# Order of work in the first pass of layer 0's self attention: exponentials two rounds sooner, context keys in every second round, their maxima last, parts by a two-operand maximum

## The chip, the cores and the metric

The kernel runs on one core of one Trainium2 chip. A core has engines with queues of their own: TensorE multiplies matrices (PE in the profile, with its weight loads as PEld) and writes to PSUM; VectorE (DVE), ScalarE (ACT) and GpSimd (POOL) work elementwise or reduce; SyncE (SP) mostly issues DMA transfers. Each engine takes its instructions in order and waits on semaphores for the others. The metric is the device time of one launch in microseconds; 1% of it here is 21.9 us.

## The reference

Four transformer blocks run one after the other on x, 8 batches of 256 tokens with 320 channels, with a context of 120 tokens. The change touches the first block, whose attentions quantise their operands. Cut to that block's attention:

```python
def fq_sym(x, bits=8):                       # symmetric, one step for the whole tensor
    qmax = 2.0 ** (bits - 1) - 1.0
    delta = jnp.maximum(jnp.max(jnp.abs(x)), 1e-08) / qmax
    return jnp.clip(jnp.round(x / delta), -qmax - 1.0, qmax) * delta

def fq_zero(x, bits=8):                      # for weights of the softmax, all positive
    levels = 2.0 ** bits - 1.0
    delta = jnp.maximum(jnp.max(x), 1e-08) / levels
    return jnp.clip(jnp.round(x / delta), 0.0, levels) * delta

def attention(x, ctx, Wq, Wk, Wv, Wo, bo, heads):      # 20 heads of 16
    q, k, v = fq_sym(x @ Wq), fq_sym(ctx @ Wk), fq_sym(ctx @ Wv)
    ...                                                # to [b, heads, tokens, 16]
    scores = jnp.einsum('bhnd,bhmd->bhnm', q, k) * dh ** (-0.5)
    w = fq_zero(jax.nn.softmax(scores, axis=-1))
    out = jnp.einsum('bhnm,bhmd->bhnd', w, v)
    return out.transpose(0, 2, 1, 3).reshape(b, n, c) @ Wo + bo

h = layer_norm(x, ln1_g, ln1_b)
x = x + attention(h, h, Wq1, Wk1, Wv1, Wo1, bo1, heads)                               # self
x = x + attention(layer_norm(x, ln2_g, ln2_b), ctx, Wq2, Wk2, Wv2, Wo2, bo2, heads)   # cross
x = x + geglu_ff(layer_norm(x, ln3_g, ln3_b), Wff1, bff1, Wff2, bff2)
```

The three steps `delta` of q, k and v need maxima over the whole tensor, and so does the step of the softmax weights. The largest weight of a row of scores is 1 over its sum of exponentials once the row's maximum is taken off, so the step of the weights needs the smallest such sum of all rows. That is why each attention goes over its scores twice: the first pass finds row maxima and sums, the second pass computes the weights again, rounds them and multiplies them with v.

## The kernel before

Everything stays on the chip; x lies in SBUF for the whole kernel. Layer 0's attentions are two objects of the class `Quant`, `s` (self) and `c` (cross). Heads lie in 5 groups of four, each head in 32 rows. The order of work comes from three places. Generators emit their instructions in steps, and `weave` takes one step of each live generator per turn; a turn is called a round here, and each generator has a round in which it starts. The framework then places waits and orders instructions within each engine's queue, by its own estimate, around that order; `behind` (line 293) ties an instruction's place to that of another without a wait. Pools of buffers set the rest: three PSUM pairs (`pair`, tile pf, 128x2x512 floats), two PSUM banks (`bank`, pa).

Self attention begins with `project_all`, which makes q, k and v of the 8 batches (the weights were loaded by `load`, q first, then k, v and o). `steps` turns the three maxima into steps. `whole` rounds q and k of a batch to whole numbers, batch 0 on VectorE and GpSimd, batches 1 and 2 on ScalarE (`whole_by_act`), batches 3 to 7 on GpSimd (`whole_all(3)`), which goes on with v (`whole_v`, lines 1391 to 1404) and adds a bias to x. The first pass then weaves four generators (line 1669), with n = 10 units per batch, a unit being one group of heads and one half of its four heads:

- `tops_all`, from round 0. One unit per round: four score products (L1453) into a PSUM pair, and a negated maximum over the keys of each row on VectorE (L1456). After a batch's tenth unit its maxima, 128x40 numbers, are split into three bf16 parts whose sum is the number: a cast (L1473), a subtraction (L1475), cast, subtraction, cast. In the third unit of the next batch (`i == 2`) TensorE transposes the parts (L1464) and ScalarE copies them to `nTs` (L1467).
- `sums_all`, from round n + 4 = 14. One unit per round: `exps` computes the scores of the unit again with keys in the rows (L1497), adds the maxima out of `nTs` by a second product with a selecting matrix, also L1497, and ScalarE takes exponentials (L1504). Products with `place` (L1519) add them over the keys; per batch, ScalarE copies the sums (L1524) and VectorE takes their minimum (L1525).
- `whole_all(3)`, from round 0, on GpSimd.
- `c.keys_all`, from round 7: the eight batches' keys of the cross attention, one per round: six products of the context with Wk2 (L120, two passes each) into a PSUM pair and a copy by ScalarE (L1274).

`c.top` then takes each key tile's absolute maximum on VectorE (L1214), `weight_steps` computes the step of the weights, and the second pass follows (`out_all`). The cross attention later runs the same `tops_all` and `sums_all` with n = 6 units and its sums from round n + 4 = 10; its own `whole_all` runs beside.

Of the kernel before, what the change touches and what calls it, by code (L numbers as in the profile page):

```python
# [14 lines left out]
ALU = mybir.AluOpType  # L15
# [4 lines left out]
B, N, C = 8, 256, 320  # L20
# [1171 lines left out]
class Quant:  # L1192
# [18 lines left out]


    def top(self, i, b, src):
        self.k.nc.vector.tensor_reduce(  # L1214
            self.am[: src.shape[0], i, b : b + 1], src, AX.XY if i == 2 else AX.X, ALU.max, apply_absolute_value=True
        )

# [220 lines left out]
    def tops_all(self):  # L1438

        k, nc, nk = self.k, self.k.nc, self.nk  # L1440
        held = None
        for b in range(B + 1):
            if b < B:
                negm = k.small.tile([P, 4, G, TPB], F32, tag="negm", name="negm")
            for i, (gs, h) in enumerate(self.units):
                if b < B:
                    s = k.pair()
                    for n, g in enumerate(gs):
                        for t in range(TPB):
                            for j in range(2):  # L1450
                                kt, q = self.operands(b, g, 2 * h + j)
                                o = (n * TPB + t) * nk
                                nc.tensor.matmul(  # L1453
                                    s[:, j, o : o + nk], q[:, t * P : (t + 1) * P], kt, start=True, stop=True
                                )
                    nc.vector.tensor_reduce(  # L1456
                        negm[:, 2 * h : 2 * h + 2, gs[0] : gs[-1] + 1, :].rearrange("p j g t -> p j (g t)"),
                        s[:, :, : len(gs) * TPB * nk].rearrange("p j (t k) -> p j t k", k=nk),
                        AX.X, ALU.max, negate=True,
                    )  # L1460
                if i == 2 and held is not None:
                    ps = k.ps_a.tile([P, 1024], BF16, tag="a", name="pt")
                    for t in range(TPB):
                        nc.tensor.transpose(  # L1464
                            ps[:, t * P : (t + 1) * P], held[:, t].rearrange("p j r -> p (j r)"), k.ident16
                        )
                    nc.scalar.copy(k.nTs[:, b - 1, :], ps[:, :N])  # L1467
                if i == len(self.units) - 1 and b < B:
                    held = k.npx
                    src = negm.rearrange("p j g t -> p t j g")  # L1470
                    for n in range(3):
                        part = held[:, :, :, G * n : G * (n + 1)]
                        nc.vector.tensor_copy(part, src)  # L1473
                        if n < 2:
                            nc.vector.tensor_tensor(src, src, part, ALU.subtract)  # L1475
                yield
                if b == B and i == 2:
                    return

    def exps(self, b, gs, heads, kind):  # L1480
# [156 lines left out]
def kernel(ctx: ExitStack, tc: tile.TileContext, a, out):  # L1637
    k = Kernel(ctx, tc, a, out)
    with ExitStack() as es:
        k.open_flow(es)  # L1640

        def load(layer, q, kk, v, o, row):
            plain = layer == "L0"
            w = {"q": k.weight_q("q", f"{layer}_xattn_{q}", q == "Wq2")}
            if kk is not None:
                w["k"] = (k.weight_q if plain else k.weight_k)("k", f"{layer}_xattn_{kk}")
                w["v"] = k.weight_v("v", f"{layer}_xattn_{v}")
            if o is not None:
                w["o"] = k.weight_o("o", f"{layer}_xattn_{o}")
            return w, k.bias_row(k.fk, row)  # L1650

        w, brow, loaded, w3 = {}, {}, {}, {}
        dram = es.enter_context(tc.tile_pool(name="ahead", bufs=1, space=bass.MemoryType.DRAM))
        ff = ExitStack()
        with tc.tile_pool(name="l0", bufs=1) as pool:
            k.open_quant(pool)
            with tc.tile_pool(name="l0_keys", bufs=1, side="right") as kpool:
                s = Quant(k, pool, kpool, 0, *load("L0", "Wq1", "Wk1", "Wv1", "Wo1", 0), False)
                k.load_ctx()
                s.project_all()  # L1660
                c = Quant(k, pool, pool, 1, *load("L0", "Wq2", "Wk2", "Wv2", "Wo2", 1), True)
                s.steps()
                for _ in s.whole(0, True):
                    pass

                s.whole_by_act(1)
                s.whole_by_act(2)
                n = len(s.units)
                k.weave((0, s.tops_all()), (n + 4, s.sums_all()), (0, s.whole_all(3)), (7, c.keys_all()))
                for b in range(B):  # L1670
                    c.top(1, b, c.kk[b])
                s.weight_steps()
                v = c.values_all()
                for _ in range(2):
                    next(v)
                k.weave((0, s.out_all()), (8, c.queries_all()), (5 * B + 4, islice(v, 3)))
            fp = ff.enter_context(tc.tile_pool(name="w_ff1", bufs=1, side="right"))
            context = ExitStack()
            k.open_context(context.enter_context(tc.tile_pool(name="context", bufs=1, side="right")), dram)
            ahead = k.context_steps()  # L1680
            next(ahead)
            loaded["w"] = [k.weight_ff1(fp, "L0_xattn_Wff1")]
            brow["ff0"] = k.bias_row(k.fk, 2)
            w["self"], brow["self"] = load("L1", "q1", "k1", "v1", "o1_w", 3)
            c.steps()
            next(ahead)
            for _ in c.whole(0, True):
                pass
            n = len(c.units)
            k.weave(  # L1690
                (0, c.tops_all()), (n + 4, c.sums_all()), (0, c.whole_all()), (5, v),
                (1, k.paced(islice(ahead, 20), 1)),
            )
            c.weight_steps()

            def rest():
                yield from ahead
                context.close()
                with tc.tile_pool(name="ahead_last", bufs=1, side="right") as pool:
                    yield from k.weights_last_steps(pool, dram)  # L1700

            k.weave((0, c.out_all()), (0, k.paced(rest(), 1)))
            fp2 = ff.enter_context(tc.tile_pool(name="w_ff2", bufs=1, side="right"))
            loaded["w"].append(k.weight(fp2, "ff2", "L0_xattn_Wff2"))
# [118 lines left out]
```

## Time and profile before

| what | value |
|---|---|
| median of 3 runs | 2194.03 us (2193.57 to 2208.99) |
| span of the profiled execution | 2202.1 us |
| busy share: PE, DVE, ACT, POOL | 92%, 51%, 38%, 15% |
| first score product of the first pass | 108.07 us |
| GpSimd busy in it | 109.3 to 188 us |
| last maxima, last sum of exponentials | 240.80 us, 257.92 us |

The stage by stretches: the microseconds in which each engine was busy, and the mean clock that TensorE was granted (1.00 is full).

| stretch, us | length | PE | DVE | ACT | POOL | clock |
|---|---|---|---|---|---|---|
| 108 to 133 | 25 | 21.33 | 22.45 | 11.03 | 23.60 | 0.77 |
| 133 to 188 | 55 | 43.86 | 43.92 | 33.78 | 54.96 | 0.84 |
| 188 to 240 | 52 | 47.56 | 45.51 | 39.63 | 0.00 | 0.97 |
| 240 to 258 | 18 | 17.62 | 2.20 | 16.60 | 0.00 | 1.00 |

A row of the timeline gives the start, the duration, engine, line and operation, the tile written and the one read, and how many instructions it merges; the bracket is idle time before it and what ended it. [...] The chain of waits is followed back from the last instruction to whatever released each, so its shares say which work stood on the path.

### The profile page before, as it was taken

How to read it: one execution, taken by the hardware profiler on the slowest of the kernel's cores; microseconds unless marked ns; L12 is line 12 of the kernel's file. 1: busy time of each engine (PE TensorE's matmuls, PEld its weight loads, DVE VectorE, ACT ScalarE, POOL GpSimd, SP SyncE). 2: the span in 40 equal slices, each digit the busy share in tenths (PEclk: the TensorE clock that was granted, in tenths of full speed). 3: DMA queues.
4: the chain of work that ended last, by engine and by line, in shares of the span. 5: the costliest groups of instructions: out<-in, count | busy, mean ns of one | idle time of the engine just before them, and what ended most of it. 6: DMA issues, size and time to landing. Idle time of an engine off the chain costs nothing.

```text
span 2202.1 us, 38254 instructions
## 1 busy us (share of the span) xinstructions
PE 2036.4 (92%) x16415; PEld 1194.6 (54%) x16415; DVE 1112.6 (51%) x1698; ACT 833.3 (38%) x1259; POOL 330.5 (15%) x358
## 2 busy tenths in 40 slices
PE   7888889898889999999999998899999999999997
PEld 5643345554444465465555555544555655666664
DVE  5388687445651222235555567621121666546565
ACT  3456888367542121124444444311201333222221
POOL 3194033723010000000000010100000100000100
PEclk9989889898899999999999999999999999999999
DMA  4000000642120000020000101100000120000000
GB/s 118 20 12 2 2 1 1 174 111 57 52 85 14 1 0 1 1 93 2 2 2 22 28 25 36 47 1 0 1 0 1 24 68 23 19 16 26 23 19 16
DMA packets 79303, 63.21 MB, mean 29 GB/s; under 512 B 48410, under 2 KB 68318, under 8 KB 78622
## 3 DMA queue, kind: packets, MB, share of 16 engines
q1 hardware_dynamic: 75070, 57.06, 9.4%
q10 hardware_dynamic: 4064, 3.71, 0.6%
q8 instruction: 129, 2.11, 0.4%
q14 instruction: 40, 0.33, 0.0%
HBM read 42.61 MB, written 17.37 MB: 27 GB/s over the span
## 4 chain that ended last, share of the span: by engine, by line
PE 73%; DVE 15%; issue 4%; ACT 4%; POOL 2%; DMA 2%; SPq 0%; ACTq 0%; DVEq 0%; POOLq 0%
PE pf L594 13%; PE pf L120 11%; PE pf L132 9%; PE pa L120 7%; PE pa L456 6%; PE pf L439 4%; PE pa L594 3%; PE pf L139 3%; DVE negm L1456 3%; PE pf L394 3%; PE pf L736 3%; DVE rs L464 3%; PE pf L1497 2%; PE pa L1519 2%; DVE negm L401 2%
## 5 line engine op out<-in xcount | busy, mean ns | idle before, releaser
L445 ACT ACTIVATE e<-pf 128x1024 f32<-128x1024 f32 (+2 forms) x176 | 158.5, 946 | 220.1 <-PE pf L439 213.1
L401 DVE TENSOR_REDUCE negm<-pf 128x4 f32<-128x1024 f32 (+4 forms) x224 | 188.1, 887 | 97.9 <-PE pf L394 97.9
L594 PE MATMUL pf<-xTf,ff 128*128 128x512 f32 x512 | 230.8, 597 | 6.2 <-DVE negm L401 5.2
L464 DVE RECIPROCAL rs<-pa 128x256 f32<-128x256 f32 x88 | 152.3, 1745 | 143.5 <-PE pa L456 143.5
L1504 ACT ACTIVATE e<-pf,sc_s 128x1024 f32<-128x1024 f32 x160 | 169.8, 1118 | 48.7 <-PE pf L1497 44.8
L1456 DVE TENSOR_REDUCE negm<-pf 128x4 f32<-128x1024 f32 (+2 forms) x128 | 143.3, 1151 | 69.6 <-PE pf L1453 58.2
L619 DVE SCALAR_TENSOR_TENSOR hT<-pf,cols_sb,gl 128x512 f32<-128x512 f32 x64 | 48.0, 751 | 256.4 <-ACT gl L618 254.1
L120 PE MATMUL pf<-ff,hT 128*128 128x320 f32 x640 | 174.4, 434 | 0.0
L594 PEld LDWEIGHTS pf<-xTf,ff 128*128 128x128 f32 x512 | 94.3, 190 | 125.4 <-issue 118.5
L120 PEld LDWEIGHTS pf<-ff,hT 128*128 128x128 f32 x640 | 120.9, 190 | 55.5 <-issue 6.1
L618 ACT ACTIVATE gl<-pf,cols_sb 128x512 f32<-128x512 f32 x64 | 44.0, 689 | 247.8 <-PE pf L594 247.8
L439 PE MATMUL pf<-qT,kT 32*128 32x256 f32 (+1 forms) x1280 | 122.1, 410 | 9.1 <-DVE negm L401 7.5
L394 PE MATMUL pf<-kT,qT 32*128 32x120 f32 (+1 forms) x1920 | 113.1, 326 | 18.6 <-ACT e L445 18.3
L487 POOL TENSOR_TENSOR xb<-x_sb,brow 128x640 f32<-128x640 f32 x24 | 37.0, 1543 | 563.8 <-DVE x_sb L493 555.4
L120 PE MATMUL pa<-o,oT 128*128 128x320 f32 x352 | 105.7, 441 | 15.2 <-DVE oT L465 15.2
L394 PEld LDWEIGHTS pf<-kT,qT 32*128 32x128 f32 x1920 | 83.0, 186 | 58.4 <-ACT e L445 27.5
L647 POOL TENSOR_TENSOR xb<-x_sb,brow 128x640 f32<-128x640 f32 x16 | 25.0, 1563 | 573.8 <-DVE x_sb L652 528.2
L1497 PE MATMUL pf<-Q,K 32*128 32x256 bf16 (+1 forms) x960 | 90.5, 295 | 21.7 <-DVE negm L1456 11.5
L456 PE MATMUL pa<-e,v 128*32 128x256 f32 (+1 forms) x1280 | 106.1, 391 | 2.3 <-ACT e L445 1.7
L1606 DVE TENSOR_SCALAR w<-e 128x1024 bf16<-128x1024 f32 (+2 forms) x128 | 89.2, 703 | 32.3 <-ACT e L1504 31.1
L132 PE MATMUL pf<-xT,q 128*128 128x256 f32 x384 | 100.5, 391 | 0.4 <-ACT e L445 0.2
L439 PEld LDWEIGHTS pf<-qT,kT 32*128 32x128 f32 (+1 forms) x1280 | 68.4, 182 | 55.5 <-DVE negm L401 26.9
(291 smaller groups left out, 3439.2 us busy)
## 6 DMA issues: line engine op xcount, KB each, us to landing
ff<-in_L_xattn_Wff_dram SPq DMA_DIRECT2D x1, 2560.0 KB
qT<-nT SPq DMA_DIRECT2D x160, 4.0 KB
ff<-in_L_xattn_ff_w_dram SPq DMA_DIRECT2D x1, 2560.0 KB
out_dram<-x_sb SPq DMA_DIRECT2D x16, 160.0 KB
kd_cross<-kst SPq DMA_DIRECT2D x8, 300.0 KB
vd_cross<-vst SPq DMA_DIRECT2D x8, 300.0 KB
vd_both<-vst SPq DMA_DIRECT2D x8, 300.0 KB
kT<-kd_cross SPq DMA_DIRECT2D x8, 300.0 KB
```

The lines of the kernel that those rows point to most:

```text
L120: self.nc.tensor.matmul(out, l, r, start=i == 0, stop=i == len(pairs) - 1)
L132: self.nc.tensor.matmul(o, *t[c], start=start and c == 0, stop=stop and c == n - 1, skip_group_check=True)
L394: nc.tensor.matmul(s[j // 2][:, j % 2, o : o + nk], qT[r : r + PAD, g, t * P : (t + 1) * P], kT[r : r + PAD, g, :nk], start=True, stop=True,)
L401: nc.vector.tensor_reduce(negm[:, n, 2 * i : 2 * i + 2, g0 : g0 + len(gs), :].rearrange("p j g t -> p j (g t)"), sv[:, :, :, k0:k1], AX.X, ...
L439: nc.tensor.matmul(s[j // 2][:ks, j % 2, o : o + N], kT[r : r + PAD, g, c * ks : (c + 1) * ks], qT[r : r + PAD, g, :], start=True, stop=True,)
L445: nc.scalar.activation(e[:ks, 2 * i : 2 * i + 2, :n], s[i][:ks, :, :n], AF.Exp, scale=scale)
L456: nc.tensor.matmul(o[j * PAD : (j + 1) * PAD, what * N : (what + 1) * N], w, es[g][:ks, j, c * N : (c + 1) * N], start=first and c == 0 an ...
L464: nc.vector.reciprocal(rs, o[:, N:])
L594: ins = nc.tensor.matmul(*args, **kw)
L1456: nc.vector.tensor_reduce(negm[:, 2 * h : 2 * h + 2, gs[0] : gs[-1] + 1, :].rearrange("p j g t -> p j (g t)"), s[:, :, : len(gs) * TPB * n ...
L1497: nc.tensor.matmul(s[at // 2][:ks, at % 2, o : o + N], l, m, start=not shift and o == 0, stop=shift and o + N == n, skip_group_check=True,)
L1504: nc.scalar.activation(e[:ks, :, :n], ps[:ks, :, :n], AF.Exp, scale=self.sc[:ks, 9:10])
```

## The change

Six edits:

1. In `load`, k's weight is loaded ahead of q's, with the memsets that go with it, for every layer that loads both here.
2. `c.keys_all` starts in round 2 and takes every second round (`paced(..., 1)` yields once more after each step), so in rounds 2, 4, ..., 16 instead of 7 to 14.
3. `sums_all` of the self attention starts in round n + 2 = 12.
4. In `tops_all` the transposes are emitted in the second unit of the next batch (`i == 1`), for both attentions, and the generator ends a round earlier.
5. The three bf16 parts are written by a `tensor_tensor` maximum of the source with itself in place of a `tensor_copy`, for both attentions.
6. The eight maxima of the context keys (`c.top`) are tied behind the last maxima of scores (`self.reduced`), so that VectorE runs them after those.

```diff
     def top(self, i, b, src):
-        self.k.nc.vector.tensor_reduce(
+        return self.k.nc.vector.tensor_reduce(
             self.am[: src.shape[0], i, b : b + 1], src, AX.XY if i == 2 else AX.X, ALU.max, apply_absolute_value=True
         )
...
-                    nc.vector.tensor_reduce(
+                    self.reduced = nc.vector.tensor_reduce(
                         negm[:, 2 * h : 2 * h + 2, gs[0] : gs[-1] + 1, :].rearrange("p j g t -> p j (g t)"),
...
-                if i == 2 and held is not None:
+                if i == 1 and held is not None:
                     ps = k.ps_a.tile([P, 1024], BF16, tag="a", name="pt")
...
                     for n in range(3):
                         part = held[:, :, :, G * n : G * (n + 1)]
-                        nc.vector.tensor_copy(part, src)
+                        nc.vector.tensor_tensor(part, src, src, ALU.max)
                         if n < 2:
                             nc.vector.tensor_tensor(src, src, part, ALU.subtract)
                 yield
-                if b == B and i == 2:
+                if b == B and i == 1:
                     return
...
-            w = {"q": k.weight_q("q", f"{layer}_xattn_{q}", q == "Wq2")}
+            w = {}
             if kk is not None:
                 w["k"] = (k.weight_q if plain else k.weight_k)("k", f"{layer}_xattn_{kk}")
+            w["q"] = k.weight_q("q", f"{layer}_xattn_{q}", q == "Wq2")
+            if kk is not None:
                 w["v"] = k.weight_v("v", f"{layer}_xattn_{v}")
...
-                k.weave((0, s.tops_all()), (n + 4, s.sums_all()), (0, s.whole_all(3)), (7, c.keys_all()))
+                k.weave((0, s.tops_all()), (n + 2, s.sums_all()), (0, s.whole_all(3)), (2, k.paced(c.keys_all(), 1)))
                 for b in range(B):
-                    c.top(1, b, c.kk[b])
+                    k.behind(c.top(1, b, c.kk[b]), s.reduced)
                 s.weight_steps()
```

## The prediction

> **What bounds the kernel now.** The page first: TensorE is busy for 92% of the span, so a gain has to shorten the path that feeds it, and the change touches one stage only. That stage is the first pass of layer 0's self attention, from the first score product at 108.07 us to the last sum of exponentials at 257.92 us: 150 of 2202 us, 6.8%. I call one turn of its weave a round; 80 rounds of maxima (10 for each of 8 batches) overlap with 80 rounds of exponentials that start 14 rounds later. The chain of waits of that stretch comes next, its first line being shares by line:
>
> ```profile
> by line: DVE negm L1456 31.8%; PE pa L1519 19.2%; PE pf L1497 15.0%; DVE npx L1473 8.6%; PE pf L1453 7.7%; PE pf L120 5.7%; ACT e L1504 5.2%; DVE negm L1475 2.3%; issue 1.6%; PE pt L1464 1.4%; DVE am_c L1214 1.2%; DVE K L1358 0.4%; ACT sums
> ```
>
> The maxima on VectorE (L1456) carry the most, and L1473, a cast of 128x40 values, carries 8.6% of 150 us = 12.9 us. The busy table by stretches (L1473 alone) says where:
>
> ```profile
> 108.00:133.00 25.00, 1.72 (x3) 0.77 0.00 1
> 133.00:188.00 55.00, 11.00 (x9) 0.84 0.10 12
> 188.00:240.00 52.00, 1.70 (x9) 0.97 0.01 2
> 240.00:258.00 18.00, 0.58 (x3) 1.00 0.01 2
> ```
>
> The columns are the stretch, its length, the casts' busy time with their number, and the granted clock. After 188 us a cast takes 0.19 us; before it twelve take 12.72 us, 10.4 more than 12 x 0.19. GpSimd works without a break from 109.3 to 188 us and not at all from there to 240 us. The timeline of VectorE and GpSimd shows one of these casts:
>
> ```profile
> 160.46 0.34 DVE L1473 CAST npx<-negm 128x40 bf16<-128x40 f32 x1
> 160.83 0.23 DVE L1475 TENSOR_TENSOR negm<-negm,npx 128x40 f32<-128x40 f32 x1
> ...
> 161.74 1.57 POOL L1391 TENSOR_SCALAR tv<-V,sc_s 128x640 f32<-128x640 f32 x2
> 162.62 2.95 DVE L1473 CAST npx<-negm 128x40 bf16<-128x40 f32 x1
> 163.26 2.26 POOL L1394 MEMSET V<- 128x1280 bf16 x2
> ```
>
> The cast of 162.62 ends at 165.57, as the memset ends at 165.52. The subtraction between the casts (L1475, two SBUF operands, the same 128x40) takes 0.23 us beside a GpSimd TENSOR_SCALAR. First parts of a batch begin at 141.98, 160.46, 176.79, 196.77, 211.46, 226.14 and 240.84 us: a clean batch takes 14.69 us, the three contended ones 18.48, 16.33 and 19.98, 10.7 more than three clean ones.
>
> **The changed parts.** Sums are against the 2202.1 us span; the median of the runs shown is 2194.03, 0.4% less, and I subtract the same microseconds from it.
>
> *Cast to maximum.* All 24 operations of the stage (and 24 in the cross pass) become two-operand operations on one source. No row shows this very form; the nearest is L1475: eight in 120-188 us take 2.32 us, 0.10 each above 0.19, and the single delayed one (144.37, 0.85 us) ends with GpSimd's L1352 (144.28 to 145.18). Lower bound: no wait at all, -10.7; upper: no better than the casts, 0 (worse is a rival below). I take L1475, nearest in operands, shape and time: 3 parts x 0.10 = 0.3 of each contended batch stays, so -10.7 + 0.9 = **-9.8**. Two stretches of half clock, 146.9-150.4 and 181.1-191.3, follow long casts and are in those intervals.
>
> [...]
>
> *Transposes a round earlier.* They now stand in TensorE's queue after the scores of the next batch's second unit and before an exponentials' group, where before they stood one round on. They wait for the fifth part operation, which VectorE runs after the first unit's maxima. In the clean batch at 211.46 those maxima end at 213.49, the part at 213.58, and the group went at 213.54, released by the same maxima. Now it waits for the part (0.04 to 0.1 more) and the two transposes (0.22): 0.3 us later. Transposes leave a later place worth 0.22, so 0 to 0.3, taken 0.2, for six batches: **+1.2**. Behind them queue the exponentials and ScalarE. In the cross pass the parts of 476.80 end at 477.91 and the second unit's scores run at 480.0: 2 us of cover, 0; its casts' excess is off the chain, 0.
>
> *Keys in every second round from round 2, their maxima last, exponentials at round 12.* Before, six rounds of maxima at 1.13 us are followed by eight that each carry a key product:
>
> ```profile
> 124.91 1.60 PE L120 MATMUL pf<-ctxT,k 128*128 128x120 f32 x12
> ...
> 125.07 0.53 DVE L1473 CAST npx<-negm 128x40 bf16<-128x40 f32 x1
> 125.50 1.21 DVE L1456 TENSOR_REDUCE negm<-pf 128x4 f32<-128x1024 f32 x1
> ```
>
> There a round costs 1.85 to 2.2 us, for 1.60 + 0.39 of TensorE and 1.13 + 0.44 (L1214) + parts on VectorE; the first exponential is at 131.50. After: three rounds of scores (108.07 to 109.9), a key product at half clock to 112.9 (the row of 115.65 took 2.92), then two rounds and a key in 2 x 0.39 + 1.60 = 2.4 us, beside 2.26 of maxima. Rounds 3 to 10 are four such pairs, plus 1.3 for a second cold product: 123.8. Two more maxima, five parts (1.2) and transposes give the first exponential near 127, a lead of 4.5 us. Two key products now fall among exponentials: 5.5 rounds at 2.83/2 = 7.8, plus 3.2, put the second batch's parts at 139 instead of 141.98: **-3.0**. Bounds: 0 if the half clock of 136.7-143.5 returns longer, -5 if it stays away. The keys' eight maxima (8 x 0.44 = 3.5 us) leave this stage. Wk2's loads pass Wq2's on SP, and its memsets those on POOL; the old order's last load is done by 108 us, the first key product is due at 109.9, and Wq2 is used in the next pass: 0, with 1.9 us of margin.
>
> *End of the stage.* Two rounds fewer of exponentials alone. ScalarE bounds them: 8.20 us for eight, 1.03 each, so -2.1. Against it, the last batch's five parts have five key maxima among them, 5 x 0.44 = 2.2 us. The last maxima end at 240.80, so parts at +3.3, transposes at +3.4, sums 0.5 and scores until the first exponential at +4.7. ScalarE was done with its two at 243.95 and would copy until 244.3 (+3.5): 1.1 idle (0 to 2.2). Net **-1.0**. The other three maxima lie under 16 us of idle VectorE.
>
> *Start.* Wk1's loads pass Wq1's. TensorE already waits 0.29 us for Wk1's last at 23.95; now Wq1's lands there, and one product of 0.59 us stands behind it: 0 to +0.6, taken **+0.6**.
>
> Sum: -9.8 + 1.2 - 3.0 - 1.0 + 0.6 = -12.0. What is late next is the loop of the clean batches, maxima 1.24, group 0.61, sums 0.57, scores 0.34, 2.83 us for two rounds, which the change leaves alone.
>
> **Rivals.**
> 1. *The new operation waits for every GpSimd instruction in progress.* For: the row at 144.37. Against: the other seven. One wait of 0.9 us, the length of L1352, above the clean time for each of twelve is 10.8: against the casts' 10.4 excess this cancels the gain, leaving -2.2 + 0.4 = -1.8: no change, 2192.2.
> 2. *The keys stage stays at half clock.* The clock went to half at 106.0 and came back at 119.6, after a window full of 128-row key products; now scores lie between them. Six further cold products x 1.3 = 7.8: -4.2, 2190. For: 112-116 us, scores alone, stayed at half. Against: keys and scores fill TensorE.
> 3. *Slower: the two-operand part is held through several GpSimd instructions.* Place: twelve parts before 188 us. The casts at 162.62 and 179.68 waited 2.8 and 3.2 us. Two GpSimd instructions of 0.9 each, 1.8 a part, cost 21.6 - 10.4 = +11.2, with the other -2.2: +9, 2203. It decides from a mean wait of (10.4 + 2.2)/12 = 1.05 us; L1475 shows 0.10.
> 4. *More*: all half-clock stretches behind the first batch vanish, tail and keys at their bounds: -10.7 - 5 - 2.1 = -17.8, 2176.
>
> That the change doesn't do what it says is excluded: transposes, key products and maxima stand in the new places in the built order.
>
> **How the numbers follow.** Forecast 0.66 (2177 to 2187 alone), rivals 0.10, 0.08, 0.07 and 0.09. The time is 2194.03 - 12.0 = 2182.0. The range, 2175 to 2193, takes in the fourth rival's 2176 and the first two; outside are the slower rival and tails. 1% (21.9 us) is what a measurement of this kernel can tell: faster by that needs more than the fourth rival, 0.05; slower 0.04; within 0.91.
>
> **What would show it.** L1473 becomes a TENSOR_TENSOR of 0.2 to 0.3 us throughout, its chain share falls from 12.9 to some 3 us; first parts are about 15 us apart from the second batch on; the first exponential starts near 127; the last sum ends near 246; the transposes near the end wait for maxima of keys. Operations of 1 us and more before 188 us would make the main term wrong; keys of 2.9 us past 120 us the second.

## The result, and the profile after

The changed kernel takes 2209.32 us (median of 20 runs, 2202.19 to 2217.05) against 2200.22 us of the kernel before in the same comparison (20 runs, 2193.57 to 2215.93): ratio 1.0041, 95% interval 1.0026 to 1.0055. Two further comparisons gave 1.0030 (1.0013 to 1.0048) and 1.0024 (1.0003 to 1.0045). So it is 6 to 9 us slower by the medians, where 12 us faster was predicted; 2209 lies outside the predicted range. The forecast's base, 2194.03 us, was the median of three runs; the twenty here put it 6 us higher. Three slow executions, of 2388.80, 4554.42 and 5827.90 us (w3_part_first, before and w2_parts_keys below), are left out of every mean here.

The chain of waits of the first pass in the profile after (span 2212.2 us, time 2213.96), its line of shares:

```profile
by line: DVE negm L1456 36.1%; PE pa L1519 18.4%; PE pf L1497 15.4%; PE pf L1453 8.2%; PE pf L120 7.6%; DVE npx L1473 4.4%; DVE negm L1475 2.5%; ACT e L1504 2.2%; issue 1.7%; PE pt L1464 1.5%; DVE am_c L1214 1.4%; ACT L1549 0.8%; DVE K L135
```

L1473, now the two-operand maximum, has fallen from 8.6% to 4.4%. Its busy table by stretches (length, busy time with the number of operations, granted clock, and two columns on the DMA queues):

```profile
108.00:133.00 25.00, 1.53 (x3) 0.77 0.00 1
133.00:188.00 55.00, 3.33 (x9) 0.84 0.10 12
188.00:240.00 52.00, 1.84 (x9) 0.95 0.01 2
```

Twelve contended parts take 4.86 us instead of 12.72, as the forecast's main term wanted. But the clock of these stretches is no better (0.77 and 0.84, as before), and the stage is 2 us longer, 152.3 instead of 150.4 us from the first score product to the minimum of the last sums (L1525). The timeline where the first batch's parts are transposed shows what is new:

```profile
127.89 0.90 POOL L1355 TENSOR_SCALAR tq<-Q,sc_s 128x768 f32<-128x768 f32 x1
128.06 0.80 DVE L1473 TENSOR_TENSOR npx<-negm 128x40 bf16<-128x40 f32 x1
...
128.89 0.85 DVE L1475 TENSOR_TENSOR negm<-negm,npx 128x40 f32<-128x40 f32 x1
129.77 0.20 DVE L1473 TENSOR_TENSOR npx<-negm 128x40 bf16<-128x40 f32 x1
...
130.03 0.28 PE L1464 MATMUL pt<-ident,npx 128*128 128x128 bf16 x2 [1.16 <-DVE npx L1473]
```

TensorE stands idle for 1.16 us until the fifth part (L1473 at 129.77) is made. The table by stretches of one clock window each, 3.41 us (busy time of PE, PEld, DVE, ACT and POOL, then the granted clock and the DMA queues) shows what follows:

```profile
125.10:128.51 3.41, 2.33 (x26) 1.78 (x23) 3.41 (x6) 0.33 (x1) 3.41 (x3) 1.00 0.00 0
128.51:131.93 3.42, 1.74 (x23) 0.70 (x23) 2.87 (x5) 1.56 (x3) 3.42 (x3) 1.00 0.00 0
131.93:135.34 3.41, 2.97 (x15) 1.67 (x14) 0.88 (x1) 2.50 (x3) 3.41 (x2) 0.50 0.02 5
135.34:138.75 3.41, 3.41 (x24) 2.55 (x26) 0.93 (x1) 0.53 (x2) 3.41 (x4) 0.50 0.00 0
138.75:142.17 3.42, 3.42 (x27) 0.86 (x23) 1.52 (x2) 1.04 (x1) 3.42 (x2) 0.50 0.00 0
142.17:145.58 3.41, 3.41 (x20) 3.02 (x22) 0.00 (x0) 1.57 (x2) 3.41 (x4) 0.50 0.00 0
145.58:149.00 3.42, 3.21 (x52) 1.44 (x52) 3.22 (x3) 1.94 (x2) 3.42 (x2) 1.00 0.86 93
```

A window with 1.74 us of work on TensorE is followed by four at half clock, in which TensorE is never idle after the first and VectorE mostly is. The second batch's parts come at 149.43 us, 41.2 after the first score product; before it was 33.9.

The other 8 of the 10 us between these two profiles lie outside the stage: from the end of the cross attention's first pass to the feed-forward the changed kernel took 136.2 us, the one before 128.4, with the same instructions in the same order. The group table of 600 to 650 us (count, then minimum/median/maximum in ns) shows it; of the changed kernel's first profile:

```profile
L120 PE MATMUL pf<-ctxT,wk_ca x12: 379/632/796, 615.6 to 624.6; 128*128 128x256 f32 x4, 64*128 64x256 f32 x4, 128*64 128x256 f32 x2, 64*64 64x256 f32 x2
```

and of its third profile (w6_after below):

```profile
L120 PE MATMUL pf<-ctxT,wk_ca x12: 376/403/483, 614.5 to 619.9; 128*128 128x256 f32 x4, 64*128 64x256 f32 x4, 128*64 128x256 f32 x2, 64*64 64x256 f32 x2
```

The same products run at half clock in the one (granted clock 0.50 from 616.65 to 630.2 us) and at full clock in the other (1.00 from 609.4 to 631.8). So one pair of profiles can't be subtracted here, and the experiments had to find what is the kernel's and what the execution's.

### The profile page after: what moved, and what is told of

It is laid out like the page before. It is cut to its first block, busy times and chain, and to the rows that moved or that the text cites. A ratio compares the mean times of both kernels' runs of the same rounds, so it can differ in the third digit from the quotient of the medians.

```text
span 2212.2 us, 38252 instructions
## 1 busy us (share of the span) xinstructions
PE 2046.6 (93%) x16415; PEld 1200.5 (54%) x16415; DVE 1105.4 (50%) x1698; ACT 832.5 (38%) x1259; POOL 330.4 (15%) x358
## 4 chain that ended last, share of the span: by engine, by line
PE 73%; DVE 15%; issue 4%; ACT 4%; POOL 2%; DMA 1%; ACTq 0%; SPq 0%; DVEq 0%; POOLq 0%
PE pf L594 13%; PE pf L120 11%; PE pf L132 9%; PE pa L120 7%; PE pa L456 6%; PE pf L439 4%; PE pa L594 3%; DVE negm L1456 3%; PE pf L139 3%; PE pf L394 3%; PE pf L736 3%; DVE rs L464 3%; PE pf L1497 2%; PE pa L1519 2%; DVE negm L401 2%
## 5 line engine op out<-in xcount | busy, mean ns | idle before, releaser
L401 DVE TENSOR_REDUCE negm<-pf 128x4 f32<-128x1024 f32 (+4 forms) x224 | 188.0, 886 | 97.1 <-PE pf L394 97.1
L464 DVE RECIPROCAL rs<-pa 128x256 f32<-128x256 f32 x88 | 152.3, 1745 | 143.6 <-PE pa L456 143.6
L120 PE MATMUL pa<-o,oT 128*128 128x320 f32 x352 | 105.7, 441 | 14.9 <-DVE oT L465 14.9
L1504 ACT ACTIVATE e<-pf,sc_c 120x1024 f32<-120x1024 f32 (+1 forms) x96 | 89.3, 980 | 32.9 <-PE pf L1497 31.5
```

What stands on the lines that cost most here:

```text
L120: self.nc.tensor.matmul(out, l, r, start=i == 0, stop=i == len(pairs) - 1)
L401: nc.vector.tensor_reduce(negm[:, n, 2 * i : 2 * i + 2, g0 : g0 + len(gs), :].rearrange("p j g t -> p j (g t)"), sv[:, :, :, k0:k1], AX.X, ...
L464: nc.vector.reciprocal(rs, o[:, N:])
L1504: nc.scalar.activation(e[:ks, :, :n], ps[:ks, :, :n], AF.Exp, scale=self.sc[:ks, 9:10])
```

## The experiments

Two measures made the runs comparable. Each timed execution comes with its span and mean granted clock. Span times clock, the time it would have taken had the same TensorE cycles run at full clock, was 2138.1 us with a standard deviation of 2.4 over the 360 executions of the comparisons for which both are on record, while their spans went from 2186 to 2226 us. Most of what these kernels differ by is therefore time at half clock ("lost clock": span times one minus clock). The changed kernel lost 67.5 us (44 executions, mean span 2206.9), the one before 61.8 (150 executions, 2199.2): 5.7 of the 7.7 us. And each profile's first pass was cut in three: the join (first score product to the second batch's parts), the middle (to the eighth batch's parts) and the tail. All in us; "lost" is the stage's time at half clock, halved. The ratios rest on 11 or 12 executions of a kernel (20 in the first comparison of the changed one), the columns behind them on one profile each, and in w3_part_first and w5_part_first one kernel took 140.5 and 150.0 us. So a single row is weak evidence for a stage, and means below are of times, each against the kernel before in the same comparison.

| run | edits | ratio to before (95%) | stage (lost) | join | middle | second cross pass |
|---|---|---|---|---|---|---|
| before, the profile of the forecast | none | | 150.4 (16.0) | 33.9 | 98.9 | 128.4 |
| b2_before | none | | 144.8 (12.1) | 33.1 | 94.1 | 134.7 |
| b3_before | none | | 145.8 (13.7) | 33.1 | 95.1 | 126.9 |
| y3_load | 1 | 1.0004 (0.9978 to 1.0030) | 142.6 (10.2) | 34.0 | 91.0 | 128.3 |
| changed | all | 1.0041 (1.0026 to 1.0055) | 152.3 (17.0) | 41.2 | 94.5 | 136.2 |
| x1_after | all | 1.0030 (1.0013 to 1.0048) | 151.9 (14.7) | 40.0 | 95.3 | 134.7 |
| w6_after | all | 1.0024 (1.0003 to 1.0045) | 150.3 (13.8) | 41.4 | 92.4 | 128.1 |
| x2_parts | 5 | 0.9978 (0.9961 to 0.9995) | 140.9 (8.0) | 34.6 | 88.7 | 130.0 |
| y1_parts_last | 5, 6 | 1.0013 (0.9989 to 1.0037) | 142.6 (9.5) | 32.2 | 92.3 | 128.3 |
| x3_keys | 2, 6 | 1.0019 (0.9996 to 1.0043) | 145.6 (10.8) | 32.7 | 94.8 | 134.7 |
| w2_parts_keys | 2, 5 | 0.9988 (0.9968 to 1.0008) | 142.3 (8.5) | 34.2 | 90.5 | 128.4 |
| z2_parts_keys | 2, 5, 6 | 0.9980 (0.9961 to 0.9999) | 138.6 (2.7) | 31.1 | 89.4 | 128.2 |
| w1_exps_back | all but 3 | 0.9987 (0.9963 to 1.0012) | 142.6 (4.4) | 31.2 | 92.8 | 129.1 |
| y2_parts_sooner | 3, 4, 5 | 0.9996 (0.9975 to 1.0017) | 140.4 (6.5) | 35.0 | 89.5 | 136.3 |
| x4_no_keys | all but 2 | 1.0000 (0.9982 to 1.0018) | 141.8 (8.3) | 33.3 | 92.0 | 129.2 |
| y4_keys_first | all, keys in rounds 2 to 9 | 1.0048 (1.0028 to 1.0069) | 150.5 (15.6) | 36.8 | 97.1 | 126.9 |
| z1_transposes_back | all but 4, exponentials at 13 | 1.0009 (0.9989 to 1.0030) | 149.0 (15.3) | 36.5 | 93.8 | 130.1 |
| w3_part_first | all, fifth part first | 1.0030 (1.0005 to 1.0054) | 140.5 (6.5) | 34.7 | 89.2 | 136.3 |
| w5_part_first | the same | 1.0005 (0.9976 to 1.0034) | 150.0 (15.5) | 36.2 | 97.2 | 126.7 |
| w4_best | 2, 5, 6, fifth part first | 0.9977 (0.9960 to 0.9995) | 144.0 (8.7) | 31.7 | 94.2 | 134.8 |

**The changed kernel again (x1_after, w6_after), no edit.**

> The changed kernel once more, for a second profile. Two theories of why it is slower. Theory K (keys): the key products between the exponentials starve TensorE, the clock falls to half, and the second batch's parts come 10 us later than forecast; the rest of the program only shifts. Theory L (later passes): the first pass ends within 2 us of before, and the loss comes from half clock in layer 0's second cross pass (606 to 650 us), where both kernels run the same instructions. By K the second profile again has parts of the second batch near 149.4, the last sum near 260 and a length of 606-to-648 that can be either; by L the stretch around 606 to 650 us again shows half clock of some 14 us, and the distance to before there is again about 8 us. If that half clock is chance, it is absent here, and the span falls to about 2203.

> The changed kernel, a third profile. If its first pass is typically long, 149 to 154 us with a fall of the clock near 132; if the two before were chance, 141 to 147. The second cross pass is 127 to 130 us or 134 to 137 with about even odds, as in any kernel here, by where the clock's windows fall; a third time 134 or more would speak for a cause in the change. The mean span is 6 to 9 us over before.

The long first pass is typical (152.3, 151.9, 150.3), and its cause stands at the same place each time: a wait of L1464 for the fifth part (1.16, 1.55 and 1.16 us), then four windows at half clock from 131.9, 132.0 and 134.2 us. It isn't where the clock's windows happen to lie (their grid is shown in the last section): the first score product stands 3.23, 2.02 and 0.23 us ahead of the next point of that grid. The second cross pass isn't the change's: 136.2, 134.7 and 128.1 here, 128.4, 134.7 and 126.9 before. Theory L, which looked best in the first pair of profiles, falls. The mean time of w6_after was 4.2 us over before, less than the 6 to 9 expected; x1_after's was 7.4 over.

**The kernel before again (b2_before, b3_before), no edit.**

> The kernel before, a second profile. Theory B (baseline): the profile that the prediction was worked out from is an unusual execution; its first pass took 150.4 us from the first score product to the last sum of exponentials, 16.0 of them lost at half clock, while the kernel with edit 1 alone, which has the same instructions in this stage, took 142.6 us. By B the stage takes 142 to 147 us here and its twelve contended parts have less than 8 us of excess over 0.19 each. Against B: 149 to 152 us again, then edit 1 must act on the stage.

> The same once more, a third profile: by theory B 142 to 147 us for the stage, against it 149 to 152. The second cross pass (128 or 135 us in the profiles so far) is expected at either value in any kernel, by where the boundaries of the 3.41-us clock windows fall.

Theory B holds: 144.8 and 145.8 us. The table of L1473 by stretches in b2_before:

```profile
108.00:133.00 25.00, 1.63 (x3) 0.72 0.01 1
133.00:188.00 55.00, 3.72 (x9) 0.91 0.10 12
```

The casts take 5.35 us (4.63 in b3_before), not 12.72. The two long ones that the forecast names, at 162.62 and 179.68 (2.95 and 3.41 us), belong to that execution.

**Edit 1 alone (y3_load).**

```diff
-            w = {"q": k.weight_q("q", f"{layer}_xattn_{q}", q == "Wq2")}
+            w = {}
...
+            w["q"] = k.weight_q("q", f"{layer}_xattn_{q}", q == "Wq2")
```

> Edit 1 alone: k's weight loaded ahead of q's. The prediction's term: 0 to +0.6, so the same as before within 2 us (mean span 2199). A rival: the order of the loads moves the start or the loads that lie beside layer 0's cross attention; then the first score product starts 1 us or more later, or the span is 3 us or more over before.

The first score product starts at 108.19 us (108.07 to 108.24 in three profiles of before): no cost of the start, no difference in the time that could be told. (The start itself lies between 107.8 and 110.1 us in the 20 profiles, with edit 1 and without.)

**Edit 5 alone (x2_parts).**

```diff
-                        nc.vector.tensor_copy(part, src)
+                        nc.vector.tensor_tensor(part, src, src, ALU.max)
```

> Edit 5 alone: the parts as two-operand maxima in both attentions, all else as before. By the prediction's main term the three contended batches fall from 18.5, 16.3 and 20.0 us to about 15 each, the last sum moves from 257.9 to 248 and the time by -9.8. By theory K the same (it blames the keys): -7 to -10. By theory L the stage ends 5 to 10 us sooner but the total may be anywhere between -10 and +5, since the later passes lose or win clock. A rival, that the operation gains nothing outside this stage's contended batches: total about -5 as the changed kernel's three contended intervals summed to 5.25 us less.

The stage is 140.9 us, four to five under the two later profiles of before, though only 1.7 under y3_load, which has before's instructions here. The mean time is 5.0 us under before's: the rival's figure, half of the main term's -9.8. How a few operations can do this is seen in one spot. In b2_before the cast that meets GpSimd's memset is held until it ends, and TensorE's next group waits 2.20 us:

```profile
171.97 2.29 POOL L1394 MEMSET V<- 128x1280 bf16 x2
172.66 1.72 DVE L1473 CAST npx<-negm 128x40 bf16<-128x40 f32 x1
...
176.33 0.39 PE L1497 MATMUL pf<-Q,K 32*128 32x256 bf16 x4 [2.20 <-DVE negm L1456]
```

The clock is at half from 176.7 to 183.5, and the batch takes 18.6 us instead of 14.7. In x2_parts the same spot:

```profile
173.84 2.27 POOL L1394 MEMSET V<- 128x1280 bf16 x2
...
174.29 0.20 DVE L1473 TENSOR_TENSOR npx<-negm 128x40 bf16<-128x40 f32 x1
...
176.41 0.39 PE L1497 MATMUL pf<-Q,K 32*128 32x256 bf16 x4 [0.65 <-DVE negm L1456]
```

The two-operand maximum, 0.20 us, isn't held by the memset, TensorE waits 0.65 us, and the clock stays. That spots like this make up the whole 5 us is not shown.

**Edits 2 and 6 (x3_keys), and with 5 (z2_parts_keys, w2_parts_keys).**

```diff
-                k.weave((0, s.tops_all()), (n + 4, s.sums_all()), (0, s.whole_all(3)), (7, c.keys_all()))
+                k.weave((0, s.tops_all()), (n + 4, s.sums_all()), (0, s.whole_all(3)), (2, k.paced(c.keys_all(), 1)))
...
-                    c.top(1, b, c.kk[b])
+                    k.behind(c.top(1, b, c.kk[b]), s.reduced)
```

> Edits 2 and 6 alone: keys in every second round from round 2, their maxima last; exponentials stay at round 14, transposes in the third unit, casts stay. Theory K: the second batch's parts come 4 to 8 us later than before's 141.98 (fewer exponentials stand between the keys than in the changed kernel, so less than its 7.5), the time +4 to +8. The prediction's own term would be 0 to -3 us. Theory L: the parts within 2 us of before, time unforeseen.

> Edits 2, 5 and 6: keys in every second round, maxima last, two-operand parts; exponentials at 14 and transposes in the third unit. Theory T: as edits 5 and 6 alone, stage 141 to 145 us, mean span within 3 us of before's. Theory K: stage 148 or more, span 5 or more over before. (Edits 2 and 6 alone took 145.6 us and 4.3 more than before.)

> Edits 2 and 5 alone (two-operand parts, keys in every second round), all else as before. By all theories the stage is 138 to 143 us; edit 6 is priced by the difference from edits 2, 5 and 6 (mean span 4.3 us under before): the prediction gave it +2.2 less what is hidden, so 0 to 2 us less here, -4 to -7 against before.

With exponentials left at round 14 the spread keys do no harm to the join: it takes 32.7 and 31.1 us with edit 6 and 34.2 without it. Theory K, that the spread keys by themselves are the loss, had wanted a later second batch in x3_keys, whose parts came 33 us after the first score product as ever. Its time agrees with K, though: x3_keys was 4.4 us over before on the mean, where K said 4 to 8, with 1 just inside the interval. With edit 5 beside them the spread keys are below before, by 4.2 us (z2_parts_keys) and 2.7 (w2_parts_keys, for which 4 to 7 was expected). So they aren't the loss of the changed kernel, and why x3_keys is not faster than before stays open. Edits 2, 5 and 6 together have the shortest first pass of the 20 profiles, at half clock up to 114.3 us and not once more within it.

**Edit 6 on edit 5 (y1_parts_last).**

> Edits 5 and 6 alone: parts as two-operand maxima, the keys' absolute maxima behind the last maxima of scores; keys at round 7, exponentials at 14, transposes in the third unit. Against the run of edit 5 alone (stage 140.9 us from first score product to last sum, mean span 5.1 us under before's). Theory C (clock): span is about 2138 us of work plus what TensorE loses at half clock, so edit 6 can only act through the clock: five key maxima among the last parts delay the last batch's exponentials by 0 to 2 us, and eight maxima less of 0.44 us in the keys' rounds give back 0 to 3; mean span within 3 us of edit 5 alone. A rival, that edit 6 is what costs the changed kernel its gain: +4 or more over edit 5 alone.

The mean time is 2.2 us over before, 7.2 more than edit 5 alone, which was measured on another chip; taken by itself that is the rival's +4 or more. But the intervals overlap (1.0013 against 0.9978), and with edit 2 the sign is the other way (0.9980 with edit 6, 0.9988 without). No price of edit 6 can be told. A key maximum does stand ahead of the last batch's parts: they begin at 233.46, 0.36 us after the last maxima.

**Edit 2 undone (x4_no_keys), and edits 3, 4 and 5 alone (y2_parts_sooner).**

```diff
-                k.weave((0, s.tops_all()), (n + 2, s.sums_all()), (0, s.whole_all(3)), (2, k.paced(c.keys_all(), 1)))
+                k.weave((0, s.tops_all()), (n + 2, s.sums_all()), (0, s.whole_all(3)), (7, c.keys_all()))
```

for the first; the second is the kernel before with the three edits.

> The changed kernel with edit 2 undone: keys again in every round from round 7. Theory K: the second batch's parts come at 137 to 142 instead of 149.4, the last sum at 249 to 253, the time 7 to 11 us under the changed kernel's and under before's. Theory L: the stage's end moves by what K says or less, and the total does not follow it. A third theory, E (early exponentials): the transposes in the second unit and the exponentials at round 12 do the harm, then the parts stay at 147 or later with the keys back in place.

> Edits 3, 4 and 5: parts, exponentials at round 12, transposes in the second unit; keys and their maxima as before. The prediction's terms for 3 and 4 are +1.2 and -2.1 to -3 without the keys: within 2 us of edit 5 alone (mean span -5 against before). If the transposes in the second unit cost more than priced, by waits of TensorE for the parts that bring the half clock in either attention, it is 3 us or more over edit 5 alone, and near before.

Early exponentials and early transposes without the spread keys are no better and no worse than the kernel before (1.0000 and 0.9996), although both have the two-operand parts, which alone gave 0.9978: they give back some 4 us of mean time (y2_parts_sooner was 0.8 under before, x4_no_keys 1.0, x2_parts 5.0), and the loss of the changed kernel needs edit 2 as well. In x4_no_keys the second batch's parts came at 141.27 us, where K put them; E, which had them at 147 or later, falls.

**Keys in every round from round 2 (y4_keys_first).**

```diff
-                k.weave((0, s.tops_all()), (n + 2, s.sums_all()), (0, s.whole_all(3)), (2, k.paced(c.keys_all(), 1)))
+                k.weave((0, s.tops_all()), (n + 2, s.sums_all()), (0, s.whole_all(3)), (2, c.keys_all()))
```

> The changed kernel with the keys in every round from round 2 (2 to 9, so all eight before the first exponential at round 12) in place of every second round. Theory K (keys among the exponentials starve TensorE): the second batch's parts come at 140 to 143 as with the keys from round 7 (141.3 there) instead of 149.4, and the span falls by 6 to 9 us to that of the kernel with edit 2 undone (2198). If it is the early start of the keys that harms (half clock of the first stretch, maxima held behind key products), the parts stay at 146 or later and the span within 3 us of the changed kernel's 2207.

The worst kernel of all, 1.0048, with the second batch's parts at 145.56 us, though no key stands among the exponentials: the last key product ends at 127.7 us, the first exponential starts at 133.18. So it isn't the keys between the exponentials; early keys and early exponentials together do it. Here TensorE is short of work before a wait for the parts could matter:

```profile
130.56 0.39 PE L1497 MATMUL pf<-Q,K 32*128 32x256 bf16 x4 [1.94 <-DVE negm L1456]
131.80 0.26 PE L1453 MATMUL pf<-K,Q 32*128 32x256 bf16 x1 [0.85 <-DVE negm L1456]
```

Both waits are for maxima on VectorE, and the clock falls at 133.1 us.

**Edit 4 undone (z1_transposes_back), edit 3 undone (w1_exps_back).**

```diff
-                if i == 1 and held is not None:
+                if i == 2 and held is not None:
...
-                if b == B and i == 1:
+                if b == B and i == 2:
...
-                k.weave((0, s.tops_all()), (n + 2, s.sums_all()), (0, s.whole_all(3)), (2, k.paced(c.keys_all(), 1)))
+                k.weave((0, s.tops_all()), (n + 3, s.sums_all()), (0, s.whole_all(3)), (2, k.paced(c.keys_all(), 1)))
```

and for w1_exps_back the last line alone, with n + 4.

> The changed kernel with the transposes back in the third unit (edit 4 undone) and so the exponentials at round n + 3 = 13, one round later; all other edits stay. Theory T: the early transposes leave TensorE waiting 1.1 to 2.3 us for the fifth part wherever maxima and parts run beside GpSimd, which brings the window below the busy time that keeps the clock; then the stage falls from 152 to 143 us or so and the mean span by 6 to 9 us to 2199. Theory K (the keys in every second round do it, wherever the transposes stand): the stage stays at 149 or more and the span within 3 us of the changed kernel's.

> The changed kernel with edit 3 alone undone: exponentials at round 14 again, transposes in the second unit, keys in every second round. Theory T: the stage keeps falls of the clock behind waits of 1 us and more for the fifth part, 147 us or more, and the span 4 or more over before. Theory X: it is as edits 2, 5 and 6 (138.6 us in the one profile), at most 143, and the span within 2 us of before or under it.

With the transposes back, the join still takes 36.5 us and the clock falls at 132.3, behind waits of 1.43 and 0.85 us for maxima. With the exponentials back at 14 and the transposes left early, the join takes 31.2 us and the span is not above before's (0.9987). T was expected to show 147 us or more there and got 142.6, although TensorE waits for the fifth part as long in all as in the changed kernel (8.0 us, seven times): only the wait at the first batch's transposes is gone. By the mean time z1_transposes_back is 2.1 us over before, between the 4.2 under of edits 2, 5 and 6 and the changed kernel's 4 to 9 over. So theory X, early exponentials on top of early keys, holds for the larger part, and the rest goes to the early transposes or to the one round that the exponentials moved with them; this run can't separate the two.

**The fifth part ahead of the next batch's first maxima (w3_part_first, w5_part_first; w4_best without edits 1, 3 and 4).**

```diff
+                    if i == 0 and held is not None:
+                        k.behind(self.reduced, last_part)
...
-                        nc.vector.tensor_tensor(part, src, src, ALU.max)
+                        last_part = nc.vector.tensor_tensor(part, src, src, ALU.max)
```

> The changed kernel with one order more: VectorE takes the next batch's first maxima behind the fifth part, so the transposes' wait is shorter by up to one maximum, 1.2 us. Theory T (the wait of the early transposes for the fifth part brings TensorE under the busy time that keeps the clock): falls of the clock between 125 and 195 us go from two or three to one or none, the stage from 152 to 141 to 146 us, the mean span 5 to 9 us under the changed kernel's 2206. Theory X (the early exponentials among the keys): the stage stays at 149 or more and the span within 3 us.

> The changed kernel with the fifth part ahead of the next batch's first maxima, a second time. Theory T (the wait for the fifth part was the cause): the stage is again 140 to 145 us, and the earlier mean of +6.6 over before came from elsewhere, so the mean falls towards +2. Theory X (early exponentials among the spread keys): the short stage was chance, the clock falls at about 132 us here and stays low for 7 to 14 us, the stage takes 147 or more and the mean is again +5 to +9 over before.

> Edits 2, 5 and 6 and the fifth part ahead of the next batch's first maxima; transposes and exponentials as before. Without the early transposes the part has a round to spare, so theory T gives no gain from its order: -3 to -6 against before, as without it. If the order helps or harms by itself (the maxima it delays release TensorE's next scores), it is 3 us off that.

The first of the two profiles was T's (140.5 us, no fall of the clock between 122 and 254 us), the second X's (150.0, falls at 129.7, 150.2, 167.2 and 184.3), and the means were 6.6 and 1.9 us over before. The join is shorter in both, 34.7 and 36.2 us against 40.0 to 41.4, so the wait for the fifth part seems to be a share of it, though two profiles and a mean of w3_part_first no better than the changed kernel's don't prove it. It isn't the whole: in w5_part_first the part still comes late, since operations ahead of it are held beside GpSimd's TENSOR_SCALARs (a subtraction of 0.86 us, where one of 147.82 takes 0.20), as its timeline shows:

```profile
145.92 0.91 POOL L1355 TENSOR_SCALAR tq<-Q,sc_s 128x768 f32<-128x768 f32 x1
146.03 0.86 DVE L1477 TENSOR_TENSOR negm<-negm,npx 128x40 f32<-128x40 f32 x1
...
148.32 0.29 PE L1466 MATMUL pt<-ident,npx 128*128 128x128 bf16 x2 [1.75 <-DVE npx L1475]
149.45 0.39 PE L1499 MATMUL pf<-Q,K 32*128 32x256 bf16 x4 [0.84 <-DVE negm L1456]
```

(Lines are two on from those of the changed kernel: L1475 is the part, L1477 the subtraction.) The window around it has 1.03 us of TensorE's work, and half clock follows.

Three kernels beat both the kernel before and the changed one: edit 5 alone, edits 2, 5 and 6, and those with the part's order (w4_best), each with its interval under 1, 4 to 5 us of mean time under before. Among the three the runs don't decide.

## Why the prediction was wrong, point by point

**Cast to maximum, -9.8.** The direction was right, the size wrong, because its base was one execution. The 10.4 us of excess were 3.1 and 2.4 in two other profiles of the same kernel; the maxima in the changed kernel still have 4.6 to 4.9 us for twelve, 0.19 each above 0.2 where 0.10 was taken. The saving in busy time is thus under 1 us in a usual execution of the changed kernel, and 1.4 to 2.1 us in the profile of edit 5 alone (3.24 us for twelve); yet edit 5 alone gave 5 us, and its executions lost 56.0 us at half clock against 61.8 of before. So the gain goes by the falls of the clock that a long cast can bring, more than by the sum of the waits. In the changed kernel the middle takes 94.1 us on the mean of three profiles, against 94.8 of the four whose stage is that of before (y3_load counted): there the gain is given back.

**Transposes a round earlier, +1.2.** The clean batches agree in their length: 14.9 us instead of 14.7. The contended ones don't. The step took the case of 211.46, where the fifth part follows at once, for all batches; beside GpSimd the parts are held (0.80 us at 128.06 and 0.85 for the subtraction at 128.89, against 0.20 at 129.77). TensorE's idle time ahead of L1464 is 8.2 to 9.9 us over the stage in the three profiles. The view of this line on TensorE, 110 to 250 us, gives for the changed kernel (microseconds, times)

```profile
L1464 PE MATMUL pt<-ident,npx x16: 219/229/262, 130.0 to 246.4; 128*128 128x128 bf16 x16
its engine sat idle before it (us, times) until:
  DVE npx L1473: 8.5, 8
```

and for edits 2, 5 and 6, with the transposes in the third unit,

```profile
L1464 PE MATMUL pt<-ident,npx x16: 219/224/230, 130.9 to 232.0; 128*128 128x128 bf16 x16
its engine sat idle before it (us, times) until:
  DVE npx L1473: 1.2, 1
```

A clean batch has a wait of 0.77 us and pays 0.2 for it; a contended one has 0.8 to 2.2 us, and pays when the clock falls behind it (in the changed kernel 1.16 us, then 13.65 us at half clock). It doesn't always: w1_exps_back has the same 8.0 us of waits and one window of half clock, at 174.6 us.

**Keys, their maxima, exponentials at round 12: -3.0.** This is the step that failed, the one with the largest error. The first exponential came at 131.20 us, not near 127, and the second batch's parts at 149.43, not 139. Against the profiles of before the join is 7.3 us longer (means 40.9 and 33.5). The keys' half of the step, by itself, has the right sign: with the exponentials left at round 14 and the maxima last, the join is 31.1 to 32.7 us in four kernels, 1.8 shorter on the mean. Much of that may be the maxima: y1_parts_last, with the keys at their old place, has 32.2. The exponentials' half was wrong: added to the early keys, it makes the join 34.7 to 41.4. The step took 2.4 us for two early rounds and the clean batches' 2.83 for two later ones (its numbers add up to 138.5 rather than 139, which decides nothing). In six of the seven profiles with both edits TensorE instead waits 0.9 to 1.9 us at a time for VectorE's parts or maxima, and the clock falls behind that at 130 to 134 us. The bound "0 if the half clock returns longer" priced the return at too little: four windows, 6.8 us lost.

**End of the stage, -1.0.** From the last batch's parts to the end: 17.6 us in the four profiles whose stage is that of before, 16.5 in all three of the changed kernel, -1.1. **Start, +0.6**: under 0.2 in the kernel of edit 1 alone, less than the start differs by between profiles.

Summed by the means: join +7.3, middle -0.7, tail -1.1, +5.5 us of the 7.7 measured in the mean span; the rest is not traced, and is less than the second cross pass scatters by.

**The rivals.** The second, keys at half clock, named the right place but kept the sign of the gain; the third had the right sign and total for a wrong reason: the mean wait of a contended part was 0.19 us, far from the 1.05 from which it decides. That TensorE would wait for the fifth part in contended batches, and that early keys and early exponentials, neither of them slower than before beside edit 5, would harm together, was in none. The forecast also took 1% for what a measurement of this kernel can tell; with 20 executions of each the interval was 0.3% wide.

**What stays open.** Why early keys and early exponentials need each other to do harm isn't settled. That the exponentials then begin while VectorE still has the backlog of the half-clocked start is argued, not shown. One candidate no run tried: score products, keys and exponentials all take their room from the same three PSUM pairs, and in y4_keys_first the exponentials' product of 130.56 was released by maxima, which free a pair. Nor do the runs tell why w3_part_first had a quiet and a disturbed first pass with the same instructions, except that the boundaries of the windows lay elsewhere: in w5_part_first there is none between 119.5 and 122.9 us, while in w3_part_first, by its key products (2.92 us from 118.24, 1.60 from 122.03), the clock rose between 121.2 and 122.0.

## What to carry to other kernels

Take several profiles of the kernel before where a wait is to be priced: a long operation in one of them may be that execution's. Where TensorE is busy nine tenths of the time (92% here), don't price a wait by its length alone but ask whether the clock falls behind it, as it did here behind the window with 1.74 us of work, and keep the product that waits for a just-made operand a step behind. Two reorderings that each fill an idle stretch can empty it together: try them alone and in pairs.

## What the runs showed of the hardware

In these profiles the granted clock changed only at multiples of 3.413 us from a point that differed by execution: the 22 changes between 106 and 584 us in the first profile of before all lie at 0.16 to 0.18 us of that grid, those of the changed kernel at 2.23 to 2.26. In the 20 profiles, in windows that begin between 120 and 262 us, all 54 falls followed a window in which TensorE was busy for at most 2.41 us; of 686 windows at full clock without a fall behind them only 29 were that low. All rises followed windows of at least 3.40 us, though not each such window was followed by one. So of the 83 windows that low 54 were followed by a fall and 29 were not: 1 us without work in 3.41 was enough for half clock in some and not in others. Windows with 1.74 us of work (the changed kernel, 128.51 to 131.93) and with 1.03 (w5_part_first, 146.78 to 150.19) were followed by it.

Beside some of GpSimd's TENSOR_SCALARs the two-operand operations were held: 0.80 and 0.86 us in the rows above, where others of their lines took 0.20. Beside the memset the maximum wasn't: it took 0.20 us (x2_parts, at 174.29), where the cast took 1.72 (b2_before, at 172.66).

The second cross pass, with unchanged instructions, takes 127 to 130 us or 134 to 136, in the same kernel too (126.9 and 134.7 for before). The place of the grid sorts all 20 profiles: where the pass starts 1.07 to 1.20 us ahead of a point of the grid it takes 134.7 or 134.8 us (four profiles), at 2.44 to 2.72 us 136.2 or 136.3 (three), and elsewhere 126.7 to 130.1. These 8 us are one reason why single executions of one kernel differ by more than the change does.
